# Adding the causal mask in PSUM, visiting the experts from tile 48 on, and loading layer 1's weights in the last tiles of layer 0

## The chip, the cores and the metric

The kernel runs on one core of a Trainium2 chip. The metric is the device time of one execution in microseconds (us). Before the change three executions took 4206.21, 4192.80 and 4204.17 us, a median of 4204.17 us. A profile is one further execution, recorded instruction by instruction.

The engines are TensorE (PE; its weight loads are listed as PEld), VectorE (DVE), ScalarE (ACT), GpSimd (POOL) and SyncE (SP), which only issues transfers. PSUM is the memory that TensorE writes its products to, SBUF the working memory of all engines, DRAM the memory outside.

## The reference

Two layers work on 4096 rows (2 sequences of 2048) of 256 numbers. Each layer normalises its input and adds two branches to it.

```python
xn = _layernorm(x, axis=-1)
x = x + _L0_attn_ref(xn, ...) + _L0_ffn_ref(xn, ...)
xn = _layernorm(x, axis=-1)
x = x + _L1_attn_ref(xn, ...) + _L1_ffn_ref(xn, ...)
```

- Layer 0, attention: 16 heads, each with two causal softmax maps over head parts of 8 numbers; the second is subtracted with a learned factor; each head's output (16 wide) is scaled by its root mean square, and all go through an output projection.
- Layer 0, experts: for each row the best 2 of 8 experts by a router, `silu(gate) * up` and `down` (256 to 512 to 256), and one shared expert of the same form that every row goes through.
- Layer 1, first branch: a selective scan (state 16, inner width 512) with a short convolution before it and a gate behind it.
- Layer 1, second branch: a network of three layers, 256 to 1024 to 1024 to 256, whose weights are +1 or -1, kept as booleans.

## The kernel before

**Tiles.** Rows are kept in blocks of 512 (8 blocks, four in each sequence; `b` is the sequence, `T` the block in it). Attention goes block by block, and in each block group by group: 8 groups of two heads, four score maps each. A group of block `T` has `4T+4` key tiles of 128 keys. Counted through, layer 0 has 640 such tiles, and their number is the kernel's clock: `at` is the tile at which a group begins, and all other work is placed at a tile number.

**Two passes.** `first_pass` finds each query's largest score: for each 128 queries (`tt`) and each chunk of 512 keys (`ch`), products of queries and keys go to a PSUM tile `s1` of two score maps (L383), and VectorE takes the maximum into `mpart` (L404). `s1` has two buffers, and projections and transposes use the same two. In the last chunk, on the diagonal, the mask must be added before the maximum. The kernel does that with four more TensorE products into the same tile (L397): the identity and the mask matrix, each cut in two halves of 64 rows, in bfloat16. The halves are laid into the tile `halves` at the start by eight DMAs on SP's queue. `second_pass` recomputes the scores with keys as rows (L455), takes the exponential on ScalarE (L462), clears what is above the diagonal on POOL (L466) and multiplies by the values (L481, into `av`). A group's first pass runs beside the second pass of the group before it.

**Beside attention.** Everything else of layer 0 is cut into steps and put in the list `beside` by `place(begin, end, steps)`, sorted by tile, and issued by `until(time)` between the score products. TensorE's and SP's instructions are issued in exactly this order (`manual_schedule` for those two engines), those of the other engines are ordered by a scheduler.

- `prepare` (normalise, transpose, router logits of a block) at tiles 1 to 28, projections of queries, keys and values a little ahead of each block, the routing at tiles 30 to 44, and the scatter of rows to the experts' order, one 128-row tile every two tiles from 46 on.
- `expert_steps`: jobs of 256 rows. Sixteen jobs of the shared expert come first, then 39 of the routed experts. A job takes 5 "visits" of work: `up` (L793: gate and up products, tanh on ScalarE, two products on VectorE), `down` (L815), loads ahead of it and a store behind. Three visits lie empty between shared and routed jobs. Visit `v` is placed at tile `6 + 2.15 v`, so the 278 visits lie at tiles 6 to 604.
- The shared jobs start from the layer's input (`load_base`) and store the sum to `x1` in DRAM; `project_out` then adds a block's attention output to what `x1` holds. For the last block the sum stays in SBUF, in `late`.
- `gather`: from tile 607 to 636, for each pair of 128-row tiles, four indirect DMAs on POOL fetch the experts' results, VectorE adds them weighted to the sum (L909), takes the layer-norm statistics, and a DMA stores the sum (L919).
- `project_out(b, T)` starts 5 tiles behind the block's last group: POOL and VectorE scale the heads, and for each 128 rows a transpose (L542), a copy to `oT` on ScalarE (L548, one buffer), a product with the output weights (L553) and an addition (L561). For the last block this lies behind all tiles.

**Between the layers.** `load_layer1` is called when layer 0 has been issued. It loads all weights of layer 1: those of the scan branch and 16 pieces of `al` (L1087) on SP's queue, the booleans of the sign network on ACT's; VectorE makes two differences and two scalings of 128x1024 (L1103, L1104) and POOL four conversions (L1112). Then comes the normalisation factor of all 32 row tiles (a square root on ScalarE), and `layer1`, whose whole order is written out; its first instructions load `acc` from `x1` (L1175) and normalise it (L1183).

## Time and profile before

| what | value |
|---|---|
| median of three executions | 4204.17 us |
| profiled execution, in all | 4219.77 us |
| its span, first to last instruction | 4218.0 us |
| granted TensorE clock, mean over the span | 0.876 |
| PE, DVE, ACT, POOL busy | 88, 65, 55, 35% |
| end of layer 0's last output product | 2900 us |
| first load of layer 1's input issued | 2928 us |

Windows of the profile give, for a stretch of time, how long each engine was busy, how many instructions started, the mean clock that TensorE was granted (1.00 is full), and the transfers. The chain of waits goes back from an instruction to what released it, again and again: the time it puts down to a line is time on the path that sets the end. A timeline row gives start, duration, engine, line, operation, result and inputs, count, and in brackets how long the engine was idle before and what ended that. A group's row gives its busy time and the mean of one instruction.

### The profile page before, as it was taken

The page shows a single profiled execution, that of the slowest core. Times are in us where ns is not written, and L with a number is a line of the kernel's source. Part 1 is how long each engine was busy: PE and PEld are TensorE (multiplying, and loading weights), DVE is VectorE, ACT ScalarE, POOL GpSimd, SP SyncE. Part 2 cuts the span into 40 slices and gives each one's busy share as a digit, 9 for nine tenths or more (in the row PEclk, how much of TensorE's full clock was granted, in tenths as well). Part 3 has the DMA queues.
Part 4 walks back from the last instruction along what each step waited for, and adds up shares of the span by engine and source line. Part 5 has one row for each costly group of instructions (what it writes and reads, how often), then busy time and mean ns, then how long its engine had stood idle before and what let it go on. Part 6 is the DMA issues. An engine that isn't in the chain of part 4 may idle for free.

```text
span 4218.0 us, 57790 instructions
## 1 busy us (share of the span) xinstructions
PE 3702.2 (88%) x20976; PEld 2000.6 (47%) x20976; DVE 2757.1 (65%) x3596; ACT 2323.9 (55%) x4602; POOL 1486.9 (35%) x1859
## 2 busy tenths in 40 slices
PE   6899999999999999999999999984568778878877
PEld 3455445444544455554444444421344545545545
DVE  4357576765676445656665667642578877878887
ACT  2335455554666644554654566542665665766674
POOL 2112331100000022111000100241677877878877
PEclk7669999996999997998998999955788878989899
DMA  3223331121223132221222222231321321322331
GB/s 119 95 88 97 98 99 56 56 75 41 77 70 101 61 102 70 94 91 66 93 79 66 71 83 76 76 115 45 115 80 62 111 85 66 121 81 70 111 106 36
DMA packets 219051, 348.16 MB, mean 83 GB/s; under 512 B 32000, under 2 KB 119040, under 8 KB 218768
## 3 DMA queue, kind: packets, MB, share of 16 engines
q1 hardware_dynamic: 209440, 325.32, 24.2%
q0 software_dynamic: 6144, 16.79, 1.2%
q8 instruction: 167, 2.74, 0.3%
q10 hardware_dynamic: 3184, 2.36, 0.2%
q14 instruction: 116, 0.95, 0.1%
HBM read 260.88 MB, written 82.84 MB: 81 GB/s over the span
## 4 chain that ended last, share of the span: by engine, by line
PE 68%; DVE 12%; ACT 8%; issue 4%; POOL 3%; DMA 2%; SPq 1%; DVEq 0%; ACTq 0%; POOLq 0%
PE s L383 14%; PE av L481 14%; PE moe L793 11%; PE s L455 7%; PE moe L815 5%; PE f L1379 4%; DVE a L1532 4%; DVE mpart L404 3%; ACT a L1492 2%; POOL u L1480 2%; PE s L397 2%; PE f L1397 1%; DVE u L1532 1%; PE s L298 1%; PE m L1338 1%
## 5 line engine op out<-in xcount | busy, mean ns | idle before, releaser
L404 DVE TENSOR_REDUCE mpart<-s 128x2 f32<-128x1024 f32 (+3 forms) x1280 | 1353.2, 1063 | 631.5 <-PE s L455 292.3
L462 ACT ACTIVATE pr<-s 128x512 f32<-128x512 f32 (+3 forms) x2560 | 1247.3, 532 | 919.2 <-PE s L455 602.2
L455 PE MATMUL s<-qst,kc 34*128 34x512 f32 (+3 forms) x2560 | 1020.4, 467 | 35.3 <-ACT pr L462 19.5
L383 PE MATMUL s<-kc,qst 33*128 33x512 f32 (+3 forms) x2560 | 939.7, 447 | 57.4 <-DVE mpart L404 34.3
L466 POOL TENSOR_SCALAR_AFFINE_SELECT pr<-pr 128x128 f32<-128x128 f32 x1024 | 290.1, 293 | 1593.1 <-ACT pr L462 1580.0
L383 PEld LDWEIGHTS s<-kc,qst 33*128 33x128 f32 x2560 | 427.5, 201 | 752.0 <-issue 325.1
L481 PE MATMUL av<-pr,va 128*17 128x512 f32 (+3 forms) x5120 | 656.5, 584 | 5.2 <-POOL pr L466 3.2
L1480 POOL TENSOR_TENSOR u<-dxr,bc 128x1024 f32<-128x1024 f32 x256 | 601.1, 2368 | 37.2 <-PE y L1504 24.5
L455 PEld LDWEIGHTS s<-qst,kc 34*128 34x128 f32 x2560 | 449.5, 200 | 171.0 <-issue 89.3
L1492 ACT ACTIVATE a<-dtr,w_A 128x512 f32<-128x512 f32 x512 | 353.4, 691 | 93.1 <-DVE u L1532 71.2
L1379 PE MATMUL f<-h,w_f 128*128 128x256 f32 x2048 | 297.3, 300 | 70.1 <-DVE h L1390 31.7
L1379 PEld LDWEIGHTS f<-h,w_f 128*128 128x128 f32 x2048 | 267.4, 198 | 159.2 <-ACT h L1386 54.6
L1532 DVE TENSOR_TENSOR_SCAN a<-a,state,u 128x512 f32<-128x512 f32 x240 | 308.7, 1286 | 26.1 <-ACT a L1492 16.9
L1379 PE MATMUL f<-xhl,w_f 128*128 128x256 f32 x512 | 130.0, 387 | 175.0 <-ACT h L1386 142.7
L397 PE MATMUL s<-halves 64*128 64x128 bf16 x2048 | 283.1, 238 | 0.0
L793 PE MATMUL moe<-xT,w_gate 128*128 128x256 f32 x880 | 267.6, 430 | 0.0
L793 PE MATMUL moe<-xT,w_up 128*128 128x256 f32 x880 | 266.0, 427 | 0.0
L815 PE MATMUL moe<-w_down,hT 128*128 128x256 f32 x880 | 233.7, 412 | 0.0
L1542 POOL TENSOR_TENSOR u<-u,bc 128x1024 f32<-128x1024 f32 x96 | 227.0, 2365 | 7.7
L507 POOL TENSOR_TENSOR ao<-n 128x128 f32<-128x128 f32 x64 | 29.4, 459 | 530.5 <-DVE n L504 529.7
L1379 PEld LDWEIGHTS f<-xhl,w_f 128*128 128x128 f32 x512 | 94.7, 247 | 241.8 <-ACT h L1386 188.4
L1542 DVE TENSOR_TENSOR u<-a,bc 128x1024 f32<-128x1024 f32 x160 | 195.2, 1220 | 5.6
(196 smaller groups left out, 4201.5 us busy)
## 6 DMA issues: line engine op xcount, KB each, us to landing
kc<-kd SPq DMA_DIRECT2D x640, 64.0 KB
dxr<-dtd SPq DMA_DIRECT2D x64, 512.0 KB
dtr<-dtd SPq DMA_DIRECT2D x64, 512.0 KB
w_gate<-in_L_ffn_gate_proj_w SPq DMA_DIRECT2D x39, 512.0 KB
w_up<-in_L_ffn_up_proj_w SPq DMA_DIRECT2D x39, 512.0 KB
w_down<-in_L_ffn_down_proj_w SPq DMA_DIRECT2D x39, 512.0 KB
qst<-qd SPq DMA_DIRECT2D x256, 64.0 KB
bc<-bcd SPq DMA_DIRECT2D x32, 512.0 KB
```

The source lines that it names most:

```text
L383: nc.tensor.matmul(pt[:, i, :width], grp["q"][r : r + R + 1, pair, tt * P : (tt + 1) * P], grp["k"][ch][r : r + R + 1, pair, :width], star ...
L404: nc.vector.tensor_reduce(grp["mpart"][:, tt, 2 * pair : 2 * pair + 2, ch : ch + 1], pt[:, :, :width], AX.X, ALU.max,)
L455: nc.tensor.matmul(pt[:, lo:], grp["k"][st // 4][r : r + R + 2, pair, (st % 4) * P : (st % 4 + 1) * P], grp["q"][r : r + R + 2, pair, lo:] ...
L462: nc.scalar.activation(pr[:, j, lo:], pt[:, lo:], AF.Exp)
L481: nc.tensor.matmul(av[32 * j : 32 * j + DV + 1, lo:], vas[b, st // 4][:, st % 4, 2 * g + j // 2, :], pr[:, j, lo:], start=(st == 0), stop= ...
L793: nc.tensor.matmul(moe[:, half, :], w[:, k, m * P : (m + 1) * P], jb["xT"][:, k, :], start=(k == 0), stop=(k == KC - 1),)
L815: nc.tensor.matmul(moe[:, i, :], jb["hT"][:, m, i * P : (i + 1) * P], jb["down"][:, m, :], start=(m == 0), stop=(m == MC - 1),)
L1379: nc.tensor.matmul(pt, w[wname][:, k, m * P : (m + 1) * P], h[src][:, k, part, :], start=(k + part == 0), stop=(k + 1 + part == nk + 1),)
L1480: nc.gpsimd.tensor_tensor(u, sg["dxr", c, half], sg["bc", g][:, 0:1, :].to_broadcast([P, 2, L]), ALU.mult)
L1492: nc.scalar.activation(a[:, i, :], sg["dtr", c, half][:, i, :], AF.Exp, scale=w["A"][:, k : k + 1])
L1532: nc.vector.tensor_tensor_scan(h[:, i, :], a[:, i, :], u[:, i, :], sg["before"]["state"][:, k[i] : k[i] + 1] if sg["before"] else 0.0, ALU ...
L1542: (nc.gpsimd if aside else nc.vector).tensor_tensor(u, h, sg["bc", g][:, 1:2, :].to_broadcast([P, 2, L]), ALU.mult)
```

## The change

1. *Mask.* The products of halves go, with `halves`, the bfloat16 identity and the eight DMAs. The mask tile is kept in 32 bits, and VectorE adds it to the diagonal 128 columns of both score maps, in PSUM, before it takes the maximum.
2. *Visits.* Visit `v` is placed at tile `48 + 590 v / 278`. The order of jobs is: 12 shared jobs (blocks 0 to 5), the three empty visits, 39 routed jobs, then 4 shared jobs (blocks 6 and 7). Since a block's attention output can now come before its shared sum, whichever is first reads the layer's input and the other reads `x1`.
3. *Gather.* It begins 1.5 visits behind the routed jobs, at about tile 599, beside the last four shared jobs, and takes the 16 pairs in another order, those of blocks 6 and 7 in between. The last shared jobs add to what was gathered, take the statistics and store it.
4. *Output projection.* The transpose of the next 128 rows is issued ahead of the product of these; `oT` has two buffers.
5. *Layer 1.* At tile 640, before the last block's output projection is issued, the normalisation factors of 28 of the 32 row tiles are computed and the weights of the scan branch loaded (`load_branch`). The booleans of the sign network are loaded in layer 1, right behind the first `acc`, on SP's queue, with their VectorE and POOL conversions (`load_signs`).

```diff
@@ block_kernel
-    layer0(tc, t, x, x1, mv, rstd, ident, eps)
-    w1p = ctx.enter_context(tc.tile_pool(name="w1", bufs=1, side="right"))
-    w1 = load_layer1(tc, t, w1p, ident)
-    nc.scalar.activation(rstd, mv[:, :, 1], AF.Sqrt, bias=eps)
...
+    def behind():
+        normalisation(0, NTILE - 4)
+        pool = w1p.enter_context(tc.tile_pool(name="w1", bufs=1, side="right"))
+        load_branch(tc, t, pool, ident, w1)
+
+    layer0(tc, t, x, x1, mv, rstd, ident, eps, behind)
+    normalisation(NTILE - 4, NTILE)
@@ layer0
-        halves = new(wp, [P, 2, 2, P], "halves", BF16)
-        for i, m in enumerate((identb, mask_ts)):
-            for half in range(2):
-                for head in range(2):
-                    nc.sync.dma_start(
...
@@ first_pass.scores
-                    for half in range(2):
-                        for head in range(2):
-                            h = slice(64 * head, 64 * head + 64)
-                            nc.tensor.matmul(
-                                pt[:, head, tt * P : width],
-                                halves[h, 0, half, :],
-                                halves[h, 1, half, :],
-                                start=False,
-                                stop=half == 1,
-                            )
+                    block = pt[:, :, tt * P : width]
+                    nc.vector.tensor_tensor(
+                        block, block, mask_ts[:, None, :].to_broadcast([P, 2, P]), ALU.add
+                    )
@@ project_out
+                    src = x1 if blk in stored else x_t
...
-                oTs[i] = new(sp, [P, KC * P], "oT", bufs=1)
+                oTs[i] = new(sp, [P, KC * P], "oT", bufs=2)
...
+            steps += [lambda: turn(0)]
             for i in range(4):
-                steps += [lambda i=i: turn(i), lambda i=i: project(i)]
+                steps += [lambda i=i: turn(i + 1)] * (i < 3) + [lambda i=i: project(i)]
@@ expert_steps
-            order = [dict(j=j, shared=True) for j in range(NT // GR)]
+            order = [dict(j=j, shared=True, last=False) for j in range(2 * NSH)]
             order += [dict(j=j, shared=False) for j in range(NJ)]
+            order += [dict(j=j, shared=True, last=True) for j in range(2 * NSH, 2 * NBLK)]
@@ placing
-            when = 6 + 2.15 * visit
+        BEGIN = 48
+        def when(visit):
+            return BEGIN + (at - 2 - BEGIN) * visit / visits
...
-        begin = 6 + 2.15 * visits + 3
+        begin = when(gathered + 1.5)
+        pairs_order = [12, 0, 1, 2, 13, 3, 4, 14, 5, 6, 15, 7, 8, 9, 10, 11]
...
+        def end():
+            routed.close()
+            ended()
+        place(at, at, [end])
@@ load_signs (behind load_branch's weights before)
-        nc.scalar.dma_start(b0, t["L1_ffn_k0"].rearrange("(k p) f -> p k f", p=P))
+        nc.sync.dma_start(b0, t["L1_ffn_k0"].rearrange("(k p) f -> p k f", p=P))
...
-                nc.scalar.dma_start(b1, bits[:, h : h + 4, :])
+                nc.sync.dma_start(b1, bits[:, h : h + 4, :])
@@ layer1
+            until(segs[0]["at"] - NU + 6)
+            load_signs()
+            fp = ctx.enter_context(tc.tile_pool(name="l1_f", bufs=1))
             until(-1.5)
```

## The prediction

> **What bounds the kernel now.** I read the page first (PEclk: granted clock in tenths, 40 slices), then windows by stage, then the chain of waits inside layer 0, then single stretches of the timeline.
>
> ```profile
> span 4218.0 us, 57790 instructions
> PE 3702.2 (88%) x20976; PEld 2000.6 (47%) x20976; DVE 2757.1 (65%) x3596; ACT 2323.9 (55%) x4602; POOL 1486.9 (35%) x1859
> ...
> PEclk7669999996999997998998999955788878989899
> ...
> L397 PE MATMUL s<-halves 64*128 64x128 bf16 x2048 | 283.1, 238 | 0.0
> ```
>
> Layer 0 fills the first 2900 us. There are 640 key tiles of the second pass, four L455 products each, so the count of L455 gives the tile at any time. Windows at tiles 0 to 48, the 16-tile pause of the experts, the last tiles with experts, and the end without them (all instructions; columns PE, PEld, DVE, ACT, POOL, clock, DMA):
>
> ```profile
> 76.00:390.00 314.00, 279.49 (x1518) 158.51 (x1518) 165.24 (x338) 125.20 (x273) 54.70 (x174) 0.72 0.30 95
> ...
> 918.00:1012.00 94.00, 87.93 (x365) 38.54 (x364) 49.35 (x54) 34.23 (x72) 9.45 (x33) 0.56 0.16 51
> ...
> 2600.00:2706.00 106.00, 104.61 (x674) 51.53 (x671) 73.85 (x87) 67.54 (x138) 7.08 (x24) 1.00 0.18 55
> 2706.00:2793.00 87.00, 81.09 (x358) 31.92 (x357) 60.79 (x112) 41.16 (x85) 47.87 (x71) 0.60 0.42 118
> 2793.00:2877.00 84.00, 61.28 (x213) 17.95 (x214) 17.05 (x51) 34.21 (x67) 28.23 (x44) 0.50 0.24 75
> ```
>
> The last of these stretches again, L455 alone:
>
> ```profile
> 2600.00:2706.00 106.00, 44.39 (x117) 18.52 (x116) 1.00 0.18 55
> 2706.00:2793.00 87.00, 44.30 (x82) 19.48 (x82) 0.60 0.42 118
> 2793.00:2877.00 84.00, 32.82 (x64) 13.97 (x64) 0.50 0.24 75
> ```
>
> See two things. PE has work nearly all the time, so PE's work, divided by the granted clock, is the time. And the clock follows the experts: 1.00 with them, 0.50 to 0.60 as soon as they pause (918) or end (2706), although PE is 93% busy in 2706 to 2793. The chain from 76 to 2900 us, by line:
>
> ```profile
> by line: PE s L383 20.8%; PE av L481 20.2%; PE moe L793 16.7%; PE s L455 9.9%; PE moe L815 7.4%; DVE mpart L404 4.0%; PE s L397 2.5%; PE s L298 2.1%; issue 1.9%; PE s L496 1.5%; PE s L553 1.4%; ACT pr L462 1.3%; PE s L329 1.2%; DMA xs<-xn,r
> ```
>
> Of 2824 us the mask products hold 2.5% (71 us), the experts 24.1% (681 us, 12.4 us for each of 55 jobs), VectorE's maxima 4.0% (113 us).
>
> **1. The mask.** 512 diagonal blocks lose four L397 products each. What they cost PE shows in two like stretches at clock 1.00, four 512-wide score products from an av group to the next operation, with one masked block and with none:
>
> ```profile
> 1571.06 0.50 PE L383 MATMUL s<-kc,qst 33*128 33x512 f32 x1
> ...
> 1571.64 0.29 PE L397 MATMUL s<-halves 64*128 64x128 bf16 x2
> 1571.91 0.66 PE L781 MATMUL s<-ident,x 128*128 128x128 f32 x4
> ```
> ```profile
> 2004.86 0.50 PE L383 MATMUL s<-kc,qst 33*128 33x512 f32 x1
> ...
> 2005.53 0.70 PE L793 MATMUL moe<-xT,w_up 128*128 128x256 f32 x2
> ```
>
> 0.85 against 0.67: 0.18 us a block. The middle stage (tiles 48 to 604, 390 to 2706 us) has 1656 of the 2048 products, 414 blocks: 75 us; 74 blocks fall in tiles 0 to 48 and are taken there. For it VectorE gets 512 additions of 128x256 with a PSUM input. Nothing before writes such a sum back to PSUM; the nearest rows are n<-s at L504 and xb<-xb,s at L561, 0.42 us each: 174 us more in the middle, whose VectorE share goes from 63% (1460 of 2316 us) to 71%. That is hidden while PE does not wait for the score buffer (two of them): 34.3 us of PE's waits are for mpart, 61 waits. What isn't hidden: the chain goes through 113/1.06 = 106 of 1280 maxima, 8%; 8% of 414 additions is 14 us. Against more speaks that diagonal maxima are narrower: 0.42, 0.69, 0.96 and 1.22 us for their four widths, 0.82 in the mean, so that addition and maximum together take what one full maximum takes. I keep 15. Sum **-60**. Bounds: -116 (0.28 us a block, the length of one pair's row) and +99 (every addition waited for, 174-75).
>
> A rule in the Trainium skill speaks against this part ("VectorE: DVE Perf Modes", "Rules for kernel authors"): keep the number of chained vector operations small, each drains on its own. Priced as if every addition counted, it would make +99 of this term and some +37 of the whole.
>
> **2. Tiles 0 to 48 without experts.** PE is busy 279 us at mean clock 0.72: 201 us of work at full clock. Out go 192 of the 2640 expert products (681 x 192/2640 = 50, at 0.94 clock 47) and 74 blocks (13): 141 us are left, and PE's idle 35 us. What the clock will be is the question: at 0.50, 282+35 = 317, +3; at the old 0.72, 231, -83. Attention alone ran at 0.50 (2793) and 0.56 (918); preparation and projections bring full-array work in, so 0.55: 291, **-23**.
>
> The skill's page "TensorE: Matmul & The Clock Gate", Part 1, has the clock released by any busy stretch of about 3.4 us. By it this stage would run near full clock (141+35 = 176 us, -138, the whole -237). The rows at 2706 and 918 contradict it for these narrow products; the rows decide.
>
> **3. The clock after tile 48.** After the pause the visits came back at about 966 us and the clock only at 1010 (windows: 0.50 from 966 to 1010, 0.96 to 1100). The same 45 us at half clock now follow tile 48, where it was 1.00 before: half is lost, **+20** (0 to +40).
>
> **4. Density.** 278 visits over 590 tiles, 2.12 each instead of 2.15: 3.4 more visits, 0.7 jobs of 12.4 us in the middle, **+8**. The pause between shared and routed jobs stays at tiles 175 to 182; nothing gained.
>
> **5. Tiles 604 to 640.** 171 us before (2706 to 2877). Now experts stay until the end, the clock with them. The last expert stretch has 117 L455 products in 106 us, 3.62 us a tile: 36 tiles make 130 us. The 16 gathers (1 us each of POOL's four indirect DMAs, VectorE's sums) were there before and now lie 2.3 tiles apart. I allow 4 us for their sharing VectorE with the experts: **-37**. Bounds: -55 (the 10.8 us stall at 2809 also goes and the tiles without first pass are quicker), +20 (3.2 jobs added and the clock still falls).
>
> **6. Output projection.** The transpose of the next 128 rows goes ahead of the product; PE waits about 0.5 us for oT now (0.52 at 1566.8), in 28 places, some of them filled by other work: **-6** (0 to -14). Eight DMAs of halves (0.6 us of SP's queue each) leave the start: **-3** (0 to -5).
>
> **7. Into layer 1.**
>
> ```profile
> 2900.00 0.48 SPq L566 DMA_DIRECT2D x<-late  x1
> ...
> 2907.17 0.38 SPq L1042 DMA_DIRECT2D w_in<-in_in_projT  x1
> ...
> 2928.04 0.38 SPq L1175 DMA_DIRECT2D acc<-x  x1
> ```
>
> acc, from which all of layer 1 starts, is issued behind 26 weight DMAs on SP. Now these go in front of the last store, during the last tiles, and acc waits only for the store to land (6.98 us in the chain): 2907 instead of 2928, **-21** (-25 to 0). Cover that can fail: w_in waits for the last gathers and experts, the 16 pieces of al (0.65 us each on SP) stand before the store, and VectorE's product of al before the second output sum; if w_in starts late, all this moves onto the path, up to 20 us. The five loads of the sign matrices move from ACT's queue to SP's, behind acc, ahead of bcd; VectorE's two differences and two scalings (1.22 and 0.75 us) now stand before the first convolution, POOL's four conversions (10.6 us) before its first sum. acc to first convolution took 12 us, to POOL's first sum 32 us: both cover it. The normalisation of 28 tiles earlier costs ACT one Sqrt and two table loads of 1.28 us in the last tiles, hidden.
>
> Sum: -60-23+20+8-37-6-3-21 = **-122**. Against the profiled execution (span 4218.0, 4219.8 in all): 4098. That execution lies 15.6 us above the median of 4204.2; taken from the median, **4082**.
>
> **Rivals.**
>
> A. *The wait changes place.* VectorE's addition holds the score buffer, and PE, which no longer spends time on the mask, waits there. For it: VectorE frees PE in 270 waits of weight loads for the next scores (184.5 us, on PEld, mostly covered). Against: 37% of VectorE idle. If half the middle's additions were paid (87 us), the term is +12 instead of -60: 4154.
>
> B. *Slower: the clock falls more often.* Mean clock 0.94 means 0.50 for 12% of the middle, some 280 us. If waits on VectorE open more gaps in PE, each microsecond at 0.50 costs half. The gain of 122 is gone when 244 us more run at 0.50, a mean clock of 0.89 in the middle; with 290 us more, at 0.88, 4227. For it: once down, the clock stayed at 0.50 for 44 us from 1635, with experts running. Against: the stages with the most experts per time held 0.97 to 1.00.
>
> C. *Better.* The early stage keeps the old clock (-83) and PE gains the mask fully (-75): 4082-60-15 = 4007.
>
> **How the numbers follow.** Main case 0.60, own range 4045 to 4120 (terms 1 to 3 off by 15 to 20 each); A 0.17; C 0.14; B 0.09. Range 4005 to 4165: it takes in A and most of C and leaves out B. The measurement tells about 0.3%, 13 us. Faster: main, A (up to its worst) and C, 0.88; same 0.04; slower 0.08.
>
> **What would show it.** Right: tile 48 near 365 us; clock about 0.55 until then and 1.00 from tile 60; no L397, and additions of 0.42 us on VectorE; tile 640 about 130 us after tile 604 at clock near 1.00; acc 7 us after the last store. Wrong: PE waits for the maxima of over 80 us (A); middle clock below 0.89 (B); additions over 0.6 us; clock 0.5 in the last tiles in spite of experts.

## The result, and the profile after

| | median | executions | ratio to the kernel before, 95% interval |
|---|---|---|---|
| before | 4197.1 us | 20 (4155.5 to 4215.6) | |
| after | 4190.4 us | 20 (4173.7 to 4226.4) | 0.9991 [0.9971, 1.0011] |
| forecast | 4082 us | range 4005 to 4165 | |

The change made no difference. The profiled execution of after spans 4214.2 us (4216.2 in all), against 4218.0 before. They lie 23 and 26 us above their medians, so the two traces can be compared stretch by stretch. The page of after:

```profile
span 4214.2 us, 54768 instructions
PE 3674.2 (87%) x18928; PEld 1904.0 (45%) x18928; DVE 2949.3 (70%) x4109; ACT 2328.0 (55%) x4606; POOL 1489.7 (35%) x1859
...
PEclk6555898997998987799999899998789888889898
...
L395 DVE TENSOR_TENSOR s<-s,mask_ts 128x256 f32<-128x256 f32 x512 | 219.9, 430 | 274.4 <-PE s L383 205.3
```

2048 TensorE instructions are gone and 512 additions of 0.43 us have come. PE is busy for only 28 us less, and the clock row has lower digits in its first five slices and in slices 13, 15 and 17. Windows of after at tiles 0 to 48, 48 to 56, 56 to 604, and the two halves of the end (604 to 624, 624 to 640); columns as before:

```profile
80.00:409.00 329.00, 268.73 (x1030) 130.59 (x1029) 177.35 (x372) 117.88 (x255) 54.38 (x172) 0.51 0.26 84
409.00:449.00 40.00, 40.00 (x167) 17.56 (x166) 25.00 (x40) 17.59 (x40) 13.29 (x27) 0.60 0.19 64
449.00:2763.00 2314.00, 2210.71 (x12051) 1045.88 (x12049) 1603.16 (x2278) 1280.32 (x2704) 349.68 (x961) 0.92 0.25 79
...
2763.00:2831.00 68.00, 67.21 (x407) 30.98 (x404) 65.55 (x131) 41.98 (x90) 36.44 (x58) 1.00 0.46 134
2831.00:2891.00 60.00, 53.65 (x265) 23.94 (x263) 20.07 (x61) 37.15 (x71) 20.86 (x36) 0.94 0.35 102
```

The early stage has 488 instructions fewer on PE and takes 15 us longer, at half clock. The end runs near full clock, as forecast. The middle has lost its mask products and is not shorter.

The timeline of after, between the layers:

```profile
2885.10 0.37 SPq L1061 DMA_DIRECT2D w_in<-in_in_projT  x1
...
2913.20 0.39 SPq L562 DMA_DIRECT2D x<-late  x1
2916.20 0.37 SPq L1203 DMA_DIRECT2D acc<-x  x1
```

The weights now go out before the last store, and `acc` follows it by 3 us, where the forecast had 7.

The chain of waits of after, from 80 to 2891 us:

```profile
by line: PE s L383 20.5%; PE av L475 18.3%; PE moe L791 15.6%; PE s L449 9.2%; PE moe L813 7.5%; DVE mpart L398 6.0%; issue 2.5%; PE s L298 2.2%; PE s L490 1.5%; PE s L329 1.3%; DMA kc<-kd 1.3%; PE s L549 1.3%; DVE s L395 1.1%; ACT pr L456 
```

The 2.5% of the mask products (71 us) have gone; the maxima rose from 4.0 to 6.0% and the additions hold 1.1%, together 200 us of 2811 where it was 113. The path went from PE to VectorE, and on it 87 us came for 71.

**Step by step.** Tile starts are every fourth product of the second pass. The second column of results is from a second profile of after (taken in the experiments, span 4212.0).

| step of the forecast | forecast | first profile | second profile |
|---|---|---|---|
| lead-in before tile 0 (DMAs of step 6) | -3 | +3.7 | +1.7 |
| 2: tiles 0 to 48 | -23 | +15.6 | +11.8 |
| 3: clock after tile 48 (48 to 96) | +20 | +14.2 | +14.1 |
| 1, 4, 6: tiles 96 to 604 | -58 | +22.8 | +13.8 |
| 5: tiles 604 to 640 | -37 | -39.5 | -29.6 |
| 7: into and through layer 1 | -21 | -20.7 | -17.7 |
| sum | -122 | -3.9 | -5.9 |

Steps 3, 5 and 7 are there. The rows of steps 1 and 2 are off by 107 to 119 us together.

**Where it went.** I split layer 0 of every profile, from its start to the last score product of tile 640, into three parts that add up to its length: *work*, PE's busy time multiplied by the granted clock; *half-clock loss*, half of the busy time at clock 0.50; and *idle*, the time in which PE does nothing.

| kernel | order | mask in the first pass | work | half-clock loss | idle | layer 0 |
|---|---|---|---|---|---|---|
| before | old | products | 2423 | 285 | 166 | 2875 |
| after | new | one addition | 2351 | 330 | 211 | 2891 |
| after, second profile | new | one addition | 2358 | 310 | 218 | 2886 |

PE lost 65 to 72 us of work, and got back 25 to 45 us of half clock and 45 to 52 us of idle time. Tiles 0 to 48 took 329 and 325 us in the two profiles of after, and tiles 320 to 352, the first block of the second sequence, 201 and 188; the same stages of the other kernels stand in the second table below.

### The profile page after: what moved, and what is told of

It is laid out like the page before. It is cut to its first block, busy times and chain, and to the rows that moved or that the text cites. A ratio compares the mean times of both kernels' runs of the same rounds, so it can differ in the third digit from the quotient of the medians.

```text
span 4214.2 us, 54768 instructions
## 1 busy us (share of the span) xinstructions
PE 3674.2 (87%) x18928; PEld 1904.0 (45%) x18928; DVE 2949.3 (70%) x4109; ACT 2328.0 (55%) x4606; POOL 1489.7 (35%) x1859
## 4 chain that ended last, share of the span: by engine, by line
PE 64%; DVE 15%; ACT 7%; issue 5%; POOL 5%; DMA 3%; SPq 1%; DVEq 0%; POOLq 0%; ACTq 0%
PE s L383 14%; PE av L475 12%; PE moe L791 10%; PE s L449 6%; PE moe L813 5%; DVE mpart L398 4%; DVE a L1564 4%; PE f L1407 4%; POOL u L1508 2%; PE f L1425 2%; ACT a L1520 2%; PE s L298 2%; DVE u L1564 1%; PE m L1366 1%; DVE u L1574 1%
## 5 line engine op out<-in xcount | busy, mean ns | idle before, releaser
L383 PE MATMUL s<-kc,qst 33*128 33x512 f32 (+3 forms) x2560 | 954.9, 456 | 80.7 <-DVE mpart L398 42.0
L449 PE MATMUL s<-qst,kc 34*128 34x512 f32 (+3 forms) x2560 | 960.4, 459 | 16.4 <-ACT pr L456 15.6
L383 PEld LDWEIGHTS s<-kc,qst 33*128 33x128 f32 x2560 | 437.9, 206 | 806.6 <-issue 331.4
L449 PEld LDWEIGHTS s<-qst,kc 34*128 34x128 f32 x2560 | 420.8, 201 | 143.0 <-ACT pr L456 83.7
L395 DVE TENSOR_TENSOR s<-s,mask_ts 128x256 f32<-128x256 f32 x512 | 219.9, 430 | 274.4 <-PE s L383 205.3
```

What stands on the lines that cost most here:

```text
L383: nc.tensor.matmul(pt[:, i, :width], grp["q"][r : r + R + 1, pair, tt * P : (tt + 1) * P], grp["k"][ch][r : r + R + 1, pair, :width], star ...
L449: nc.tensor.matmul(pt[:, lo:], grp["k"][st // 4][r : r + R + 2, pair, (st % 4) * P : (st % 4 + 1) * P], grp["q"][r : r + R + 2, pair, lo:] ...
```

## The experiments

They ran in four groups of four, each group on one chip beside 19 to 25 executions of the kernel before; across groups only the ratios to before are compared. The ratios and the medians of a pair can differ by some 10 us. First the measured ratios; the split of layer 0 and two stages of the same kernels follow, from one profiled execution each.

| order | products | one addition | no mask |
|---|---|---|---|
| old, visits from tile 6 | 1 | 1.0101 [1.0063, 1.0140] | 0.9934 [0.9897, 0.9970] |
| new, visits from 48 | 1.0032 [1.0003, 1.0062] | 0.9991 [0.9971, 1.0011]; again 1.0047 [1.0017, 1.0076] | 0.9909 [0.9878, 0.9940]; again 0.9870 [0.9822, 0.9917] |
| new, visits from 6 | | 1.0132 [1.0066, 1.0198] | 0.9933 [0.9889, 0.9978] |
| new, 4 gather buffers | | 1.0029 [0.9998, 1.0059] | 0.9850 [0.9813, 0.9886] |

| kernel | work | half-clock loss | idle | layer 0 | tiles 0-48 | tiles 320-352 |
|---|---|---|---|---|---|---|
| before | 2423 | 285 | 166 | 2875 | 313.6 | 166.2 |
| old order, no mask | 2358 | 281 | 182 | 2821 | 310.3 | 165.9 |
| old order, addition | 2352 | 314 | 216 | 2882 | 323.1 | 172.2 |
| new order, products | 2426 | 284 | 180 | 2890 | 312.6 | 173.1 |
| new order, no mask | 2355 | 290 | 192 | 2836 | 302.0 | 169.7 |
| new, no mask, again | 2361 | 279 | 190 | 2830 | 301.1 | 167.6 |
| new, no mask, 4 buffers | 2358 | 272 | 189 | 2819 | 300.8 | 168.0 |
| new, addition, 4 buffers | 2356 | 320 | 219 | 2895 | 324.9 | 187.9 |
| new, addition, from tile 6 | 2359 | 345 | 224 | 2927 | 341.2 | 182.7 |
| new, no mask, from tile 6 | 2358 | 323 | 177 | 2859 | 332.8 | 172.9 |
| new, two additions | 2352 | 351 | 310 | 3013 | 339.2 | 209.3 |
| new, addition and products | 2419 | 341 | 205 | 2965 | 337.0 | 177.7 |

### The two halves of the change

The mask alone, on the kernel before (the products as in the diff above):

```diff
+                    block = pt[:, :, tt * P : width]
+                    nc.vector.tensor_tensor(
+                        block, block, mask_ts[:, None, :].to_broadcast([P, 2, P]), ALU.add
+                    )
-                    for half in range(2): ...
```

> The kernel before with the mask part of the change alone: VectorE adds the mask in PSUM, the products of halves and their DMAs are gone; visits, gathers and weights stay as they were. The prediction's own term for this was -60 (4137 beside 4197). Theory CLOCK (the products lay half in the shadow of other work and were work of the whole array that kept TensorE's clock up; without them the clock falls more often): 4190 to 4225, with a lower clock in the stages of short groups, above all tiles 320 to 352. Theory WAIT (VectorE's 0.43 us hold the score buffer and TensorE waits): 4190 to 4225 too, with TensorE's idle time ahead of the score products up by 40 us or more. Theory ORDER (the mask is a gain and the new order of the visits eats it): 4120 to 4150.

Measured: 4237.2 us, 1.0101 [1.0063, 1.0140]. By itself the new mask makes the old kernel 1.0% slower, some 42 us by the ratio and 30 by the medians. The time lies above the range of CLOCK and WAIT; ORDER, with 4120 to 4150, falls for the mask. PE's idle time in layer 0 rises by 50 us (166 to 216), on WAIT's side; tiles 320 to 352, where CLOCK looked for a lower clock, keep 0.84 beside 0.86 before.

Everything but the mask: the changed kernel with the products of halves put back.

```diff
-                    nc.vector.tensor_tensor(
-                        block, block, mask_ts[:, None, :].to_broadcast([P, 2, P]), ALU.add
-                    )
+                    for half in range(2): ...
```

> The changed kernel with the mask as products of halves again: the new order of visits, gathers, output projection and weights alone. From the traces of before and after: end of layer 0 -40, step to layer 1 -21, tiles 0 to 56 some +25, so CLOCK and WAIT expect 4150 to 4170, under both kernels. ORDER expects 4200 to 4260.

Measured: 4217.8 us, 1.0032 [1.0003, 1.0062], in ORDER's range and above the other one. The new order gains nothing either. So it is not one half that ate what the other brought: neither brought what was forecast for it. And with the new order the two masks come out alike (1.0032 with products, 0.9991 and 1.0047 with the addition); the 1.0% between them stands in the old order alone. Windows of this kernel at tiles 0 to 48, 56 to 604 and 604 to 624:

```profile
76.00:389.00 313.00, 267.63 (x1327) 139.72 (x1326) 149.98 (x299) 121.22 (x257) 54.79 (x172) 0.55 0.27 89
424.00:2739.00 2315.00, 2230.30 (x13669) 1129.56 (x13667) 1447.83 (x1873) 1279.63 (x2703) 355.14 (x964) 0.94 0.24 79
...
2739.00:2827.00 88.00, 83.47 (x455) 39.65 (x453) 62.74 (x118) 43.61 (x93) 36.77 (x61) 0.84 0.34 105
```

With products the early stage had the clock of the forecast (0.55) and stood 13 to 17 us below the changed kernel's; the end, however, was not quick here (step 5 below).

### Products without effect, and no mask

Addition and products together, the products adding zeros:

```diff
+        nc.vector.memset(halves[:, 1], 0.0)
...
+                    for half in range(2): ...
                     block = pt[:, :, tt * P : width]
                     nc.vector.tensor_tensor(
                         block, block, mask_ts[:, None, :].to_broadcast([P, 2, P]), ALU.add
                     )
```

> The changed kernel, mask added by VectorE, and in addition the four products of each diagonal block with a mask of zeros, so the sums are unchanged: TensorE's work of before comes back and VectorE's addition stays. CLOCK: the clock in tiles 320 to 352 comes back to 0.85 or more and the time is 4160 to 4205, no more than 15 above the changed kernel in spite of 2048 more products. WAIT: the products are pure cost, 512 times 0.18 us, 4250 to 4290, clock in tiles 320 to 352 no higher than in the changed kernel.

Measured: 4276.6 us, 1.0158 [1.0113, 1.0204], in WAIT's range. Over layer 0 the products give no clock back: half-clock loss stays at 341 us, and their work (some 65 us) comes on top. In one stage, however, CLOCK's sign did appear. Tiles 320 to 352 of this kernel, and of after:

```profile
1570.00:1748.00 178.00, 161.01 (x1023) 92.25 (x1024) 111.14 (x200) 74.11 (x181) 44.80 (x141) 0.86 0.26 83
```
```profile
1543.00:1743.00 200.00, 179.99 (x788) 92.05 (x786) 110.28 (x200) 73.09 (x180) 44.39 (x141) 0.71 0.24 73
```

With the products the clock is 0.86 there, and the stage is 10 to 23 us shorter than in the two profiles of after. As an account of the whole kernel CLOCK falls; whether the products help the clock in this stage stays open.

No mask in the first pass:

```diff
-                if last:
-                    block = pt[:, :, tt * P : width]
-                    nc.vector.tensor_tensor(...)
```

> The changed kernel with no mask at all in the first pass: the maximum then takes in the 128 keys of the diagonal block that lie ahead of the query. This leaves out the masking of the maxima; the second pass still clears those keys, and the softmax is divided by the same sum, so only the shift in the exponent changes. Neither products nor additions are left. WAIT: the additions' waits go, 4080 to 4130. CLOCK: TensorE's work is as in the changed kernel, so the clock in tiles 320 to 352 stays at 0.65 to 0.75 and the time at 4160 to 4190.

Measured: 4162.3 us, 0.9909 [0.9878, 0.9940], faster than both kernels. The time is in CLOCK's range and 32 us above WAIT's, but CLOCK's sign, a clock of 0.65 to 0.75 in tiles 320 to 352, is not there. Windows at tiles 56 to 604 and 320 to 352:

```profile
414.00:2687.00 2273.00, 2179.44 (x12048) 1035.14 (x12047) 1448.37 (x1875) 1277.97 (x2704) 355.14 (x965) 0.94 0.25 80
...
1493.00:1663.00 170.00, 158.62 (x791) 83.03 (x792) 88.67 (x142) 72.80 (x181) 44.73 (x141) 0.82 0.27 88
```

PE has no mask products here, as in after, and the clock is 0.94 and 0.82 where after had 0.92 and 0.71. Idle and half-clock loss are those of the products' kernel (192 and 290 against 180 and 284) and the work is 71 us less. So it is not the missing products but the addition that brings idle time and half clock.

### Both orders, and an earlier start

The old order without mask:

```diff
-                if last:
-                    for half in range(2): ...
```

> The old order, with no mask in the first pass at all: neither the products of halves nor the addition (the maxima on the diagonal are then taken over keys that come later too; the second pass still clears them). It completes a table of two orders by three masks. I split layer 0 of each profile into PE's work at full clock, time lost while PE works at half clock, and PE's idle time: before 2423 + 285 + 166 us, after 2351 + 330 + 211, new order without mask 2355 + 290 + 192. Theory GAP: the products are worth some 70 us of PE work in either order, and what eats them after the change is the addition, which opens gaps in PE and with them stretches at half clock. Then this kernel has work near 2352, idle 170 to 195, half-clock loss 275 to 305, and takes 4145 to 4170 us against 4200 before. Rival FILL: in the old order the products lay in time that PE had over anyway, so that taking them out brings nothing there: work falls by 70, but idle and half-clock loss rise by as much, 4190 to 4210.

Measured: 4173.9 us, 0.9934 [0.9897, 0.9970]: 28 us below the kernel before on its chip by the ratio, 38 by the medians. Work fell by 65, idle rose by 16. The median lies 4 us above the range of GAP and 16 below that of FILL: mainly GAP, with a small share that PE had over anyway.

The changed kernel with visits from tile 6 on, and the same without mask:

```diff
-        BEGIN = 48
+        BEGIN = 6
```

> The changed kernel with visits from tile 6 on instead of 48, spread to the same end (2.27 tiles a visit). Theory ORDER: putting the visits off cost the early stage its clock, and that is what paid for the quicker end. Then tiles 0 to 48 run at 0.65 to 0.75 again with 18 visits in them, and take no longer than the 329 us of the changed kernel although 40 us of expert work have come in; all tiles behind 56 have 7% fewer visits. The end (tiles 604 to 640 in 125 to 140 us, layer 1 in 1322 us) stays. Time 4145 to 4165. Rival DENSITY: with visits further apart the clock falls more often in the middle, and what the early stage gains is lost between tiles 56 and 604: 4180 to 4205.

> The same with no mask in the first pass (the maxima on the diagonal are taken over later keys too): new order, visits from tile 6, neither products nor addition. Theory ORDER: the new order without mask took 4162; visits from tile 6 take 25 to 45 us off that: 4115 to 4140. Rival DENSITY: 4150 to 4180. Theory GAP says of this kernel against the one with the addition that it has 15 to 25 us less of PE idle and 30 to 45 us less of half-clock loss in layer 0, FILL that it has the same.

Measured: 4259.7 us, 1.0132 [1.0066, 1.0198], and 4187.8 us, 0.9933 [0.9889, 0.9978]. Both lie above the ranges of both theories: visits from tile 6 on make the changed kernel slower, not faster. Putting the visits off costs the early stage some of its clock, but no time: the theory ORDER of these two runs falls. Window of the first at tiles 0 to 48:

```profile
80.00:421.00 341.00, 297.58 (x1201) 153.37 (x1201) 191.76 (x409) 123.22 (x273) 54.03 (x173) 0.62 0.27 86
```

The clock does rise, from 0.51 and 0.53 to 0.62, less than the 0.65 to 0.75 expected, and the stage is 12 to 16 us longer than with no experts in it. Half-clock stretches in layer 0 rise from 35 to 50. Of one pair on one chip the addition cost 72 us here; by the split, 47 of idle and 22 of half clock, where GAP expected 15 to 25 and 30 to 45.

### What a clock burst does

Eight bursts of full-array products in the early stage:

```diff
+        def burst():
+            pt = new(ps1, [P, 2, 512], "s1")[:, 0]
+            for _ in range(12):
+                nc.tensor.matmul(pt[:, :C], wo[:, 0, :P], wo[:, 0, :], start=True, stop=True)
+        for i in range(12, 48, 5):
+            place(i + 0.4, i + 0.4, [burst])
```

> The changed kernel with eight bursts of twelve 128-row products of 256 columns (0.35 us each at full clock), at tiles 12, 17, 22 and so on to 47; their result is never read. Theory GAP, the clock's part of it: the clock is recorded in stretches of 3.41 us; in the two traces it falls after a stretch in which PE was busy for less than half, and comes back only after one that 128-row products fill to eight tenths or more. By it the clock stands at 1.00 within 7 us of at least seven of the eight bursts, and then holds for 10 to 40 us, to the next gap. The mean clock in tiles 0 to 48 goes from 0.51 to 0.65 to 0.80; the stage has 136 + 34 us of work, some 55 of idle, and takes 265 to 315 us where it took 329; the whole some 20 to 50 us less than the changed kernel, 4140 to 4170. Rival LOAD: the clock follows the load over a long time, a few bursts do not move it: it stays at 0.50 to 0.57, and the stage takes 350 to 390 us, the whole 4220 to 4250.

Measured: 4246.7 us, 1.0104 [1.0066, 1.0142]. Three windows at the second burst (226.3 to 233.7 us) and the stretches about it:

```profile
193.00:223.00 30.00, 25.63 (x102) 14.39 (x102) 11.82 (x23) 8.45 (x22) 5.07 (x17) 0.50 0.28 88
223.00:230.00 7.00, 6.93 (x24) 4.79 (x25) 3.80 (x15) 4.50 (x7) 0.58 (x2) 0.50 0.01 2
230.00:240.00 10.00, 8.61 (x48) 5.44 (x46) 4.05 (x11) 3.00 (x9) 1.77 (x6) 0.98 0.08 28
240.00:263.00 23.00, 18.37 (x81) 10.67 (x80) 11.99 (x29) 7.70 (x18) 3.91 (x13) 0.51 0.34 107
```

Seven of the eight bursts began at half clock, and the clock was full 1.8 to 4.9 us after each began: the rule of the return holds. But it then held only 7 to 17 us, the rest of the burst among them, and fell in the next gap. With a mean clock of 0.64 the stage took 352 us and the whole what LOAD had expected, though not for LOAD's reason: the clock is lost to gaps, and winning it back for less than 20 us does not pay for a burst of 5 to 8 us.

### The changed kernel again, shorter trains of gathers, two additions

> The changed kernel again, for a second profile and its time beside the runs of this chip. In six other kernels of the new order tiles 576 to 640 took 260 to 276 us, against 229 in the profile of the changed kernel and 270 to 275 in the old order; five of the six have a stop of 5 to 9 us in tiles 594 to 603, in which VectorE, ScalarE and TensorE all stand still while POOL issues gathers one behind the other, and 17 to 40 us of half clock behind it. Theory STOP: the quick end in the one profile was luck, the stop belongs to the new order: a second profile shows it, with 255 to 275 us for tiles 576 to 640, and the forecast's 37 us for the end are not in the median. Rival END: the changed kernel's end is quick, 225 to 240 us again, and the stops come with the edits of the other kernels. Tiles 0 to 48 by both 315 to 335 us at a clock of 0.50 to 0.57. Time 4180 to 4205 by both.

Measured: 4234.0 us, 1.0047 [1.0017, 1.0076]; on this chip the change is a little slower, and 29 us above what both theories expected. Tiles 576 to 640 took 252.6 us, between the two theories (228.8 in the first profile). Windows at tiles 576 to 604, 604 to 624 and 624 to 640:

```profile
2634.00:2748.00 114.00, 108.00 (x585) 48.41 (x583) 82.46 (x119) 65.65 (x131) 25.88 (x39) 0.90 0.31 97
2748.00:2820.00 72.00, 70.07 (x409) 32.31 (x407) 65.69 (x130) 41.97 (x91) 35.14 (x56) 1.00 0.42 126
2820.00:2886.00 66.00, 57.55 (x262) 25.00 (x260) 19.95 (x61) 36.94 (x71) 20.87 (x35) 0.84 0.30 90
```

Four buffers for the gathered rows instead of eight, with the addition and without mask:

```diff
-                        y = pairs[pair, i, o] = new(mps[0], [P, C], "yr", bufs=8)
+                        y = pairs[pair, i, o] = new(mps[0], [P, C], "yr", bufs=4)
```

> The changed kernel with four buffers instead of eight for the gathered rows, so that at most four gathers are in flight and the next ones wait for VectorE's sums. Theory STOP, if long trains of gathers are what stops the other engines: no stop of over 3 us with gathers in tiles 590 to 640, tiles 576 to 640 take 225 to 245 us, and the whole 15 to 35 us less than the changed kernel, 4155 to 4180. Rival QUEUE: the stops come anyway, or POOL, which now waits in front of its clearing of the diagonal blocks, holds PE up instead: 4185 to 4215.

> The new order with no mask in the first pass (the maxima on the diagonal are taken over later keys too) and four buffers for the gathered rows. With eight it took 4162 us, with a stop of 8 us in tile 598. Theory STOP: 4130 to 4150. Rival QUEUE: 4155 to 4180.

Measured: 4223.4 us, 1.0029 [0.9998, 1.0059], and 4146.2 us, 0.9850 [0.9813, 0.9886]. With the addition the time is above the ranges of both, the end took 265 us and one stop of 4 us remained: STOP falls. Without mask the time is in STOP's range, but the end took 267 us, as with eight buffers (270), so the gain is not from there. This pair gives the price of the addition once more: 77 us.

The mask added twice:

```diff
+                    nc.vector.tensor_tensor(
+                        block, block, mask_ts[:, None, :].to_broadcast([P, 2, P]), ALU.add
+                    )
```

> The changed kernel with the mask added twice on every diagonal block: 512 more additions of 0.43 us on VectorE, 220 us in all, that change no result. One addition instead of none cost 28 us in this order, 63 in the old order and 72 with visits from tile 6. Theory GAP: the addition lies on the way from a score buffer's product to its release, PE waits for it in part, and the clock falls behind the gaps; the second addition does the same again: PE idle in layer 0 up by 20 to 50 us, half-clock loss up by 20 to 50, time 4225 to 4280. Rival COVER: VectorE has room in this order and the 28 us were something else (the wait for the first maxima after the mask, code, placing): 4180 to 4205.

Measured: 4353.2 us, 1.0340 [1.0304, 1.0377], 119 us over the changed kernel, more than GAP expected; COVER falls. Half-clock loss rose by 21 to 41 us, as GAP had it, idle time by 92 to 99, twice the most that it had. The largest wait of PE for the maxima, without mask, in after and with two additions, one line of each list of waits (total us, times, longest):

```profile
PE s L372 <- DVE mpart L381: 30.0, 58, 3.4
```
```profile
PE s L383 <- DVE mpart L398: 42.0, 75, 2.6
```
```profile
PE s L383 <- DVE mpart L401: 79.2, 122, 3.3
```

Over all lines of PE the waits for maxima in layer 0 are 50.5, 73.2 and 134.1 us (before: 49.4; old order with the addition: 69.2). Without mask the old order has 52.2. So one addition on each diagonal block makes PE wait 17 to 23 us more for maxima; the two pairs that ran on one chip cost 72 and 77 us in all.

### Where the addition costs

The addition only in the first block of each sequence, only in the others, and products in the first blocks with additions in the others:

```diff
-                if last:
+                if last and T == 0:
```
```diff
-                if last:
+                if last and T > 0:
```
```diff
+                if last and T == 0:
+                    for half in range(2): ...
-                if last:
+                elif last:
```

> The changed kernel with the addition in the first block of each sequence alone (128 of the 512 diagonal blocks); in the other blocks the maxima are taken over later keys too. Theory DENSE: the addition costs where every chunk is a diagonal one and PE has little beside it, in the lead-in, in tiles 0 to 32 and 320 to 352; elsewhere it lies beside other work. Then this kernel is nearly as slow as with all additions: tiles 0 to 48 at 315 to 330 us, tiles 320 to 352 at 185 to 200, the whole 40 to 60 us above the one without mask, a ratio of 0.997 to 1.005 to the kernel before. Rival SPREAD: every addition costs the same; a quarter of them costs 15 to 20 us: 0.988 to 0.995.

> The other way round: the addition everywhere but in the first block of each sequence (384 of 512), where the maxima are taken over later keys too. Theory DENSE: tiles 0 to 48 at 300 to 312 us and tiles 320 to 352 at 165 to 175, as without mask; the whole 5 to 20 us above the kernel without mask, a ratio of 0.985 to 0.994. Rival SPREAD: three quarters of the cost, 45 to 58 us above the kernel without mask: 0.997 to 1.003.

> The changed kernel with products of halves in the first block of each sequence and the addition in all others: the full mask again. Theory DENSE: 128 blocks of products are some 18 us of PE work, 20 to 30 at the clock of those stages, in place of 40 to 60 for the additions there: 15 to 40 us less than the changed kernel, a ratio of 0.990 to 0.998. Rival SPREAD: a quarter of the additions saved for 20 to 30 us of products: as the changed kernel or slower, 1.000 to 1.008.

> The new order without mask in the first pass, unchanged, as the base of the three others on their chip. It had a ratio of 0.991 to the kernel before, and 0.985 with four buffers for the gathered rows: 0.984 to 0.993 by both theories; tiles 0 to 48 at 298 to 305 us, tiles 320 to 352 at 165 to 172.

| kernel, one chip | median | ratio to before | tiles 0-48 | tiles 320-352 |
|---|---|---|---|---|
| no mask | 4155.5 | 0.9870 [0.9822, 0.9917] | 301.1 | 167.6 |
| addition in the first blocks (128) | 4189.8 | 0.9943 [0.9909, 0.9976] | 315.8 | 187.4 |
| addition in the others (384) | 4194.4 | 0.9961 [0.9929, 0.9994] | 310.9 | 169.3 |
| products in the first, addition in the others | 4195.1 | 0.9968 [0.9935, 1.0002] | 326.2 | 166.4 |

Tiles 320 to 352 with the addition in the first blocks alone, and with it in the others alone:

```profile
1525.00:1712.00 187.00, 169.21 (x788) 87.55 (x788) 106.94 (x192) 73.18 (x180) 44.53 (x141) 0.76 0.26 79
```
```profile
1491.00:1661.00 170.00, 155.91 (x792) 81.20 (x793) 91.82 (x150) 73.17 (x181) 44.64 (x142) 0.84 0.28 89
```

The same products; 17 us lie between them, at a clock of 0.76 against 0.84, for 42 more VectorE instructions. (The second profile is of the quickest of its ten executions, 30 us below their median.) The truth lies between DENSE and SPREAD. By the medians a quarter of the additions costs 34 us (0.27 us each), three quarters cost 39 (0.10 each), together 73, as much as all of them in the pairs above. The intervals of the three ratios, 0.3 to 0.5% wide to each side, do not tell these two prices apart. The stages do, in the new order: tiles 320 to 352 take 183 to 201 us in the six profiles with one addition and no products in the first blocks, and 166 to 173 in the seven without the addition there. The others are not free.

In the old order it is another picture. The same stage takes 172 us with the addition and 166 without, and 42 of the 62 us that the addition costs layer 0 there lie in tiles 96 to 604. By the split, the addition brings 6 to 9 us of idle time to tiles 320 to 352 in either order; half-clock loss stays in the old order (27 us without, 26 with) and goes from 25 to 29 us up to 39 to 55 in the new. With visits from tile 6 it stays too (35 without, 32 with), beside 11 us of idle time. So the wait costs about the same everywhere, and what comes on top depends on whether the clock falls behind it.

Products in the first blocks come out in DENSE's range and bring tiles 320 to 352 back to 166 us, but not tiles 0 to 48; against the kernel before that is no gain that its interval makes sure of.

## Why the prediction was wrong

**Step 1 failed in its price of a wait.** It charged the addition with 15 us, and step 2 put nothing on for it; measured are 56 to 76. "What isn't hidden ... 8% of 414 additions is 14" was the right size for the direct wait: 17 to 23 us more of waiting for maxima. But I charged that wait alone and put nothing on for the clock behind it, although rival B names it. In four pairs with and without the addition (old order; new, the mean of two profiles each; four buffers; visits from 6) idle time rose by 24 to 47 us and half-clock loss by 22 to 48. Layer 0 became longer by 56 to 76 us, 65 in the mean.

That the addition causes both is shown by these pairs and by the second addition. Where the half clock comes from, the traces show in the new order. In tiles 48 to 576 the clock fell 22 and 20 times without mask, 30 and 27 times with the addition, and 34 times with two. In the stretch of 3.41 us before the fall, the largest part of PE's idle time was ended by a maximum 7, 7, 16, 12 and 19 times: most of the added falls come behind maxima. In the old order there are no more falls (21 without, 20 with), only longer times at half clock (270 to 301 us); why is open.

An example in the timeline of after, without the weight loads:

```profile
221.84 0.34 PE L383 MATMUL s<-kc,qst 33*128 33x128 f32 x1
...
222.14 0.43 DVE L395 TENSOR_TENSOR s<-s,mask_ts 128x256 f32<-128x256 f32 x1 [0.51 <-PE s L449]
...
222.61 1.23 DVE L398 TENSOR_REDUCE mpart<-s 128x2 f32<-128x1024 f32 x1
...
223.98 2.05 PE L329 MATMUL s<-wv,xTb 128*128 128x256 f32 x4 [1.81 <-DVE mpart L398]
```

PE needs a score buffer, both are with VectorE, and the addition stands in front of the maximum that frees one: PE stands still for 1.81 us. VectorE's mean share (70% of the span now) says nothing of this: in tiles 320 to 352 VectorE was busy for 55% of the time, and there, in the new order, an addition cost the most.

**Step 1 was too high in its price of the products, too.** 65 to 72 us of PE work went in the whole of layer 0, where steps 1 and 2 had 75 and 13; that is 0.13 to 0.14 us a block, not 0.18. Of this, 10 to 16 us came back as idle time even where no addition replaced the products, so their removal shortens layer 0 by 54 us in the old order (2875 to 2821) and by 54 to 60 in the new (2890 to 2836 and 2830). In the forecast it was worth 99: 75 in step 1, and 13 at a clock of 0.55 in step 2. So the addition costs as much as the products that it replaces, or more.

**Step 2 failed at the idle time, and at an addition whose cost it left out.** The work that it left, 141 us, was measured as 136; the clock, 0.55 forecast, was 0.51 and 0.53; the idle time, taken over as 35, was 60 and 62. Without mask the stage took 301 to 302 us (clock 0.56 to 0.57, idle 52), near the 291 of the forecast. The step took 13 us off for the products of 74 blocks and put nothing on for their additions, which cost 23 to 28 us here.

**Rivals A and B were each right in part, and together they are the answer.** A had PE wait for VectorE, B had the clock fall in new gaps. Each had a sign of its own, waits for maxima over 80 us and a middle clock below 0.89; measured were 42 us on the line that the prediction had read (73 over all lines) and 0.92, so neither sign appeared. I had listed them as alternatives, but in the new order the one brings the other, and half of each was enough. Rival C's cheap early stage did not come.

**Steps that held, and step 5.** Step 3: +14 for +20. Step 7: -18 to -21 for -21; in all fifteen profiles of the new order the time behind tile 640 is 1316 to 1326 us, in the three of the old order 1343 to 1350. Step 5 holds in the two profiles of the changed kernel (-39.5 and -29.6; the 171 us that it started from are 168 between the first and the last score product), but tiles 576 to 604 just ahead, which the forecast left as they were, take 110 to 122 us in fourteen of the fifteen profiles of the new order, where the old order has 100 to 105. The first profile of after, with 99.8, is the exception. So the end as a whole, tiles 576 to 640, gained 42 us in that profile and 18 in the second, and with products nothing (272 against 270). In the other twelve profiles of the new order it takes 254 to 276 us. So the 37 us of step 5 are not a gain to count on; that the first profile has them is luck.

**The sum.** The forecast for layer 0 was -101 us. The products that go were worth 54 to 60 us instead of 99, the addition cost some 65 instead of 15, and the rest of the new order, forecast at -17, came to +15 with products in it (2890 against 2875), above all because tiles 576 to 640 gained nothing there. So the price of the addition is the largest of three misses, and not the only one: without any mask the new order has layer 0 at 2830 to 2836 us, 38 to 44 below before. These are single profiles, and such profiles lie up to 30 us from the median of their kernel.

**The rules that were weighed.** The page "VectorE: DVE Perf Modes" of the Trainium skill ("Rules for kernel authors") wants few chained vector operations; by it the whole came to +37 in the forecast. In the old order it spoke on the right side: the addition lost against the products by 1.0%. The rule of "TensorE: Matmul & The Clock Gate", Part 1, that any busy stretch of about 3.4 us releases the clock, is contradicted again: from 409 to 449 us of after PE was busy for all 40.00 us, at a mean clock of 0.60. The measurement decides.

**What would have been better.** Of the versions run, those without any mask in the first pass beat both kernels: 0.987 to 0.991 of the time before in the new order, 0.985 with four gather buffers as well, 0.993 in the old order and with visits from tile 6. The maximum is only subtracted before the exponential and divides out again with the sums, so in exact arithmetic the output does not change; a later key with a far larger score would push the earlier ones towards zero, and how far inputs can go there was not tried.

## What to carry to other kernels

Before work is moved to an engine that is "not the bottleneck", look for the buffer that this engine frees, and for the stretches in which the bottleneck has little else to do; a mean share over the kernel hides both. Where the matmul clock depends on PE being busy, count a wait of PE together with the slow stretch behind it: here 17 to 23 us more of waiting for one engine came with 56 to 76 us of layer 0. And when two rivals share a mechanism, price them together, half and half, before each is dismissed alone.

## What the runs showed of the hardware

**The clock falls by one rule and returns by another.** The profile records it in stretches of 3.41 us, at 1.00 or 0.50. In the traces of before and after, over the whole span, 102 stretches at full clock had PE busy for less than half of the time; 97 of them were followed by half clock; of the 1714 busier ones 51 were. Of the other way, 345 stretches at half clock had less than six tenths of their time in products with 128 rows, and none was followed by full clock, although PE was busy for over 95% of the time in 110 of them; of 89 with nine tenths or more, 87 were. Between lies no sharp bound: 36 of 165 with six to eight tenths were followed by full clock, so the "eight tenths or more" that I expected ahead of the bursts is too strict. Scores (33 and 34 rows) do not bring the clock back; experts, projections and the bursts do.

**ScalarE and VectorE can stand still beside gathers.** In tile 598 of the new order without mask, POOL issues eleven gathers one behind the other, and the two other engines stop with their operands ready (the score products ended at 2648.2 and 2649.7 us):

```profile
2649.18 0.49 PE L372 MATMUL s<-kc,qst 33*128 33x512 f32 x1
2649.23 0.95 POOL L891 DMA_INDIRECT yr<-ys,rows_at  x1 [0.31 <-issue]
...
2657.89 1.08 ACT L439 ACTIVATE pr<-s 128x512 f32<-128x512 f32 x2 [11.03 <-remote]
2657.93 1.23 DVE L381 TENSOR_REDUCE mpart<-s 128x2 f32<-128x1024 f32 x1 [8.24 <-remote]
2658.54 0.28 PEld L432 LDWEIGHTS s<-qst,kc 34*128 34x128 f32 x1 [9.18 <-ACT pr L439]
```

"Remote" means that the trace has no instruction that released them. Such stops, of 3 to 9 us for both engines together, with a mean clock of 0.57 to 0.83 in the 30 us behind them, lie in tiles 594 to 603 of thirteen of the fifteen profiles of the new order, further ones of 3 to 7 us in tiles 618 to 627 of eleven, and one of 4 us in tile 606 of the old. The first profile of after issued over 20 gathers in a row at the same place without one, and with four buffers stops of 3 to 4 us remained; what causes them stays open.
